# Last block of a four-layer perceiver kernel: the last four batches' state-space preparation moved ahead of the perceptron, its weight bytes loaded early

## The chip, the cores and the metric

The kernel runs on one core of a Trainium2 chip. A core has a matrix engine (TensorE, PE in the profile, with PEld for its weight loads), VectorE (DVE), ScalarE (ACT), GpSimd (POOL) and SyncE (SP), which here only issues DMAs. Each engine works through its own instruction list in the order in which the program puts it there, and waits for others through semaphores. Matmuls write PSUM; the other engines read it and move results to SBUF. The metric is device time in microseconds (us), lower is better.

## The reference, cut to what matters

Sixteen batches of 64 tokens with 256 features (x) go through four layers. Each has a cross-attention on a context of 1024 keys with 192 features, a second mixer and a feed-forward part. The change lies in the last layer:

```python
x = x + _L3_xattn_ref(_layernorm(x, axis=-1), ctx_768, ...)
x = x + _L3_attn_ref(_layernorm(x, axis=-1), ...)
x = x + _L3_ffn_ref(_layernorm(x, axis=-1), L3_ffn_k0, L3_ffn_k1, L3_ffn_k2, ...)
```

Its second mixer is a selective state space (Mamba style) on 512 channels with 16 states each:

```python
u, x_gate = jnp.split(x @ in_proj_w, 2, axis=-1)
u = silu(conv3(u) + conv_b)
delta, b, c = jnp.split(u @ x_proj_w, [512, 528], axis=-1)
delta = softplus(delta @ dt_proj_w + dt_proj_b)
h = jnp.exp(d_t[:, :, None] * a) * h + d_t[:, :, None] * b_t[:, None, :] * u_t[:, :, None]
y_t = jnp.einsum('bds,bs->bd', h, c_t)
y = (y + u * D_param) * silu(x_gate)
return y @ out_proj_w
```

Its feed-forward part is a perceptron whose weights are given as booleans, one byte each, meaning +1 or -1: 256 features, doubled to (x, -x), to 1024, to 1024, to 256, with relu between and a scale per layer.

## The kernel before

Tokens lie on partitions in eight tiles of 128, and `xs` holds the running x in SBUF. In the last layer three pieces of work are interleaved by hand in the order in which the program records them; PE's order is kept exactly (`manual_schedule`), that of the other engines is set by the framework from the recorded order.

- **Cross-attention**: `heads64` (L420). It first forms `wvo` from `wvT` and `wo` in `output_matrices`, and does not read `wvT` and `wo` again. It then goes through (tile, batch, group of heads); at each step it calls `breathe` four times, which here is the state space's `go`. After tile i's output, `finished(i)` sets `ssm.ready`.
- **State space**: `state_space` (L1797). A chunk is four batches, 256 tokens, two tiles, so there are four chunks, 0 to 3. `prepare(k)` is a generator: layer norm (`os`), transposes (`hTs`), eight input projections with a three-tap convolution on DVE (`up`, `ug`), Silu, the projections for b and c (`bc`) and for the step size (`du`, four of them: "dt"), then softplus, the product delta times u on POOL (L1897), and a write of both to HBM (`dus`). `items(k)` then reads them back replicated on partitions (`rep`, `bc_rep`) and does 32 items, in eight slots of four: ACT makes the decay `da` (L1938), DVE multiplies (L1944), scans (L1948) and multiplies (L1951) into one of six `x` buffers. After each slot, PE sums over the states with 16 matmuls (`add_up`, L1972); after every second slot DVE applies D and the gate (`v`, L1978). The chunk ends with an output projection added to `xs` (L89). Chunk 3 can be prepared only when the attention of the last tile is finished.
- **Perceptron**: `dense_setup` (L2009) turns the bytes into fp32 weights: w0 and w2 on DVE, w1 in eight pieces on ACT (L2021). `dense(first, 2)` does two tiles: norm and transposes (`o`, `hT`), first layer in eight groups of matmuls (`ps_h`, weights w0), second in eight groups of eight-deep matmuls (w1), third (w2) added to `xs` (L2061) and written out. Relus alternate between ACT (L2033) and DVE (L2031). It yields 15 times: 1, 4, 8 and 2.

`go` runs one piece of the current preparation, then as many items as `credit` allows: each call adds `rate`, 1.1 during the attention and 1.5 during the perceptron. After the attention `L3` (L1765) calls `dense` for tiles 0, 2, 4 and 6, with one `go` after each yield, and before each calls `go` until those tiles' state space is done:

```python
for i in range(0, NT, 2):
    while ssm.done < i + 2:
        ssm.go()
    for _ in dense(i, 2):
        ssm.go()
```

Weights come through a ring of two buffers of 7296 fp32 per partition, in the order of `packs`. The bytes of the perceptron are the last pack (`pack_L3_ffn`, L1755), whose buffer is the one that the attention's weights hold until its end; its three DMAs are issued on SP's queue. The state space's weights (`weights`, L1834) are loaded near the start of the layer.

Of the kernel before, what the change touches and what calls it, by code (L numbers as in the profile page):

```python
# [13 lines left out]
U8 = mybir.dt.uint8  # L14
AF = mybir.ActivationFunctionType
ALU = mybir.AluOpType
# [3 lines left out]
B, S, D = 16, 64, 256  # L20
# [12 lines left out]
RING = 7296  # L33
# [9 lines left out]
class Net:  # L43
# [376 lines left out]
    def heads64(  # L420
# [4 lines left out]

        nc = self.nc
        wq, wkT, wvT, wo, bo, wvo, wvo2 = self.pack()
        large = large or self.misc
        self.n_pT = 3
        qpT, hT = {}, {}  # L430
# [1318 lines left out]
    def pack_L3_attn(self):  # L1749

        self.slot()
        shape = {n: self.a[f"L3a_{n}"].shape for n in ("in", "bc", "out")}
        return self.carve(*shape["in"]), self.carve(128, 4, 512), self.carve(*shape["bc"]), self.carve(*shape["out"])

    def pack_L3_ffn(self):  # L1755
        t = self.ring.tile([128, 4 * RING], U8, tag="w", name="w")
        got, at = [], 0
        for name, c, f in (("L3f_k0", 4, 1024), ("L3f_k1", 8, 1024), ("L3f_k2", 8, D)):
            v = t[:, at : at + c * f].rearrange("p (c f) -> p c f", f=f)
            at += c * f  # L1760
            self.nc.sync.dma_start(v, self.a[name])
            got.append(v)
        return got

    def L3(self, ctx_pool):  # L1765
        tc, nc = self.tc, self.nc
        with ExitStack() as stack:

            def pool(name, **kw):
                return stack.enter_context(tc.tile_pool(name=name, reuse_waits="tile", **kw))  # L1770

            self.sb = pool("sb_L3a", bufs=1, side="right")
            ps = pool("ps_halves", bufs=1, space=PSUM)
            banks = [ps.tile([128, 2, 256], F32, name=f"halves{n}") for n in range(2)]
            self.halves, self.halves_y = ([t[:, h, :] for t in banks] for h in range(2))
            stack.enter_context(tc.manual_schedule(engines={mybir.EngineType.PE}))
            ssm = self.state_space()
            with (
                tc.tile_pool(name="sb_L3x", bufs=1, side="left", reuse_waits="tile") as self.lp,
                tc.tile_pool(name="ps_L3x", bufs=1, space=PSUM, reuse_waits="tile") as self.lps,  # L1780
            ):
                self.heads64(
                    lambda shape: self.lps.tile(shape, F32, tag="t", bufs=2, name="large"),
                    ssm.go, ssm.more, ssm.first,
                )
            ctx_pool.__exit__(None, None, None)
            self.lp = pool("sb_L3f", bufs=1, side="left")
            self.lps = pool("ps_L3f", bufs=1, space=PSUM)
            ssm.rate = 1.5
            dense = self.dense_setup()  # L1790
            for i in range(0, NT, 2):
                while ssm.done < i + 2:
                    ssm.go()
                for _ in dense(i, 2):
                    ssm.go()

    def state_space(self):  # L1797
        nc = self.nc
        N = 16
        w = []  # L1800
        s = SimpleNamespace(ready=0, done=0, rate=1.1, credit=0.0, prepared=0, started=0)
        al = self.sb.tile([128, 4 * N], F32, name="al")
        at = VEC_AT["L3a_A"]
# [30 lines left out]
        def weights():  # L1834
            for n, to in zip(("in", "bc", "out"), (w[0], w[2], w[3])):
                nc.sync.dma_start(to, self.a[f"L3a_{n}"])
            yield

        def prepare(k):
            win, wdt, wbc, _ = w  # L1840
            ug = ugs[k % 2]
            os = []
            for t in range(2):
# [1 line left out]
                mv, rs = self.norm_tile(x, 1e-5)  # L1845
                os.append(self.sb.tile([128, D], F32, tag="os", bufs=2, name="os"))
                nc.vector.tensor_scalar(os[t], x, mv[:, 0:1], rs, ALU.subtract, ALU.mult)
            yield
            hT = self.sb.tile([128, 2, CHUNK], F32, tag="hTs", name="hTs")
            for t in range(2):  # L1850
                nc.scalar.copy(hT[:, :, t * 128 : (t + 1) * 128], self.transposed(os[t]))
            yield
            up = self.act.tile([128, 4, 4, S + 2], F32, tag="hT", name="up")
            nc.gpsimd.memset(up[:, :, :, 0:1], 0.0)
            nc.gpsimd.memset(up[:, :, :, S + 1 : S + 2], 0.0)
# [16 lines left out]
                if m % 2:  # L1872
                    yield
            nc.scalar.activation(ug, ug, AF.Silu)
            yield
            yield
            ps = self.misc([32, CHUNK])
            self.mm(ps, [(wbc[:, c, :], ug[:, c, :]) for c in range(4)])
            bc = self.sb.tile([32, CHUNK], F32, tag="bc", name="bc")
# [100 lines left out]

        s.prep, s.work = weights(), None

        def go(place=None):

            if s.prep is None and s.prepared < NC and s.ready >= 2 * s.prepared + 2 and s.prepared <= s.done // 2 + 1:
                s.prep = prepare(s.prepared)
            if s.prep is not None and next(s.prep, s) is s:
                s.prepared += s.prep.gi_code is prepare.__code__
                s.prep = None
            if s.work is None and s.started < s.prepared:  # L1990
                s.work = items(s.started)
                s.started += 1
            self.spare_dve = s.work is not None
            s.credit = min(s.credit + s.rate, 2 * s.rate)
            while s.work is not None and s.credit >= 1:
                s.credit -= 1
                if next(s.work, s) is s:
                    s.work = None
# [9 lines left out]

    def dense_setup(self):  # L2009
        nc = self.nc  # L2010
        k0, k1, k2 = self.pack()

        w0 = self.lp.tile([128, 2, 1024], F32, name="w0")
        w1 = self.lp.tile([128, 8, 1024], F32, name="w1")
        w2 = self.lp.tile([128, 8, D], F32, name="w2")
        for c in range(2):
            nc.vector.tensor_tensor(w0[:, c, :], k0[:, c, :], k0[:, 2 + c, :], ALU.subtract)
        minus = self.lp.tile([128, 1], F32, name="minus")
        nc.vector.memset(minus, -1.0)
        for c in range(8):  # L2020
            nc.scalar.activation(w1[:, c, :], k1[:, c, :], AF.Identity, bias=minus, scale=2.0)  # L2021
        nc.vector.tensor_scalar(w2, k2, 2.0, -1.0, ALU.mult, ALU.add)

        sc = self.lp.tile([128, 3], F32, name="sc")
        nc.sync.dma_start(sc, self.a["L3f_s"].partition_broadcast(128))
        nc.vector.tensor_scalar(sc, sc, 2.0, None, ALU.mult)
        out = self.a["out"].rearrange("(i p) d -> p i d", p=128)

        def relu(n, out, ps, k):
            if n % 2:  # L2030
                nc.vector.tensor_scalar(out, ps, sc[:, k : k + 1], 0.0, ALU.mult, ALU.max)  # L2031
            else:
                nc.scalar.activation(out, ps, AF.Relu, scale=sc[:, k : k + 1])  # L2033

        def dense(first, tiles):
            hT = self.lp.tile([128, 2, CHUNK], F32, tag="hT", bufs=1, name="hT")
            for t in range(tiles):
                x = self.xs[:, first + t, :]
                mv, rs = self.norm_tile(x, 1e-5)
                o = self.lp.tile([128, D], F32, tag="o", bufs=2, name="o")  # L2040
                nc.vector.tensor_scalar(o, x, mv[:, 0:1], rs, ALU.subtract, ALU.mult)
                self.evict(hT[:, :, t * 128 : (t + 1) * 128], self.transposed(o))
            yield

            def layer(name, w, x, chunks, k):
                r = self.lp.tile([128, 8, CHUNK], F32, tag=name, bufs=1, name=name)
                for m in range(8):
                    ps = self.lps.tile([128, CHUNK], F32, tag="h", bufs=4, name="ps_h")
                    self.mm(ps, [(w[:, c, m * 128 : (m + 1) * 128], x[:, c, :]) for c in range(chunks)])
                    relu(m, r[:, m, :], ps, k)  # L2050
                    if m % 2 or chunks > 2:
                        yield
                return r

            r0 = yield from layer("r0", w0, hT, 2, 0)
            r1 = yield from layer("r1", w1, r0, 8, 1)
            for t in range(tiles):
                i = first + t
                po = self.misc([128, D])
                self.mm(po, [(r1[:, m, t * 128 : (t + 1) * 128], w2[:, m, :]) for m in range(8)])  # L2060
                nc.vector.scalar_tensor_tensor(  # L2061
                    self.xs[:, i, :], po, sc[:, 2:3], self.xs[:, i, :], ALU.mult, ALU.add
                )
                nc.sync.dma_start(out[:, i, :], self.xs[:, i, :])
                yield

        return dense

# [59 lines left out]
    def run(self, layers):  # L2128
# [6 lines left out]
            "L1_ffn": (self.L1_ffn, [self.pack_L1_gate]),  # L2135
            "L2_xattn_attn": (self.L2_xattn_attn, [lambda: self.pack_heads64("L2"), self.pack_L2_attn]),
            "L2_ffn": (self.L2_ffn, [self.pack_L2_gate] + [lambda e=e: self.pack_L2_expert(e) for e in range(E)]),
            "L3": (None, [lambda: self.pack_heads64("L3"), self.pack_L3_attn, self.pack_L3_ffn]),
        }
        self.packs = [p for l in layers for p in plan[l][1]]  # L2140
        self.loaded, self.at, self.ctx_n = {}, 0, 0
# [186 lines left out]
```

## Time and profile before

| | us |
|---|---|
| three runs, median (lowest to highest) | 2994.78 (2992.84 to 3002.1) |
| profiled execution | 2998.29 |
| its span, first to last instruction | 2996.5 |
| last layer's attention ends on PE | 2734.35 |
| last matmul ends | 2993.2 |
| instructions | 42608 |

The profile is of one execution. Its page gives busy time by engine (part 1), the span in 40 slices (2) and the costliest groups of instructions (5); the trace can be asked for stretches of time, waits, and lists in order of time. "Granted clock" is the share of its full clock that PE ran at. In lists of instructions a row reads: start, length, engine, line, operation, written tile <- read tiles, shape, count, and in brackets the idle time before it and what ended it. An fp32 matmul that the program wrote appears as two.

The line numbers L69, L179 and L89 belong to helpers: L69 is every ordinary matmul, L179 a transpose, L89 an addition to `xs`. The tile names tell them apart: `ps_h` is the perceptron's first two layers, `halves` everything else of the last layer.

### The profile page before, as it was taken

The page shows a single profiled execution, that of the slowest core. Times are in us where ns is not written, and L with a number is a line of the kernel's source. Part 1 is how long each engine was busy: PE and PEld are TensorE (multiplying, and loading weights), DVE is VectorE, ACT ScalarE, POOL GpSimd, SP SyncE. Part 2 cuts the span into 40 slices and gives each one's busy share as a digit, 9 for nine tenths or more (in the row PEclk, how much of TensorE's full clock was granted, in tenths as well). Part 3 has the DMA queues.
Part 4 walks back from the last instruction along what each step waited for, and adds up shares of the span by engine and source line. Part 5 has one row for each costly group of instructions (what it writes and reads, how often), then busy time and mean ns, then how long its engine had stood idle before and what let it go on. Part 6 is the DMA issues. An engine that isn't in the chain of part 4 may idle for free. (4 is left out here: it accounts for less than half of the span.)

```text
span 2996.5 us, 42608 instructions
## 1 busy us (share of the span) xinstructions
PE 2700.2 (90%) x16840; PEld 1952.8 (65%) x16840; DVE 1482.1 (49%) x3177; ACT 1022.7 (34%) x2290; POOL 308.7 (10%) x428
## 2 busy tenths in 40 slices
PE   7888997999999788989999998898998898897899
PEld 3566784666666345867777776795776666665668
DVE  3654114666666653234444444314445747658581
ACT  2331122555555211222333322122334455445330
POOL 1112223000000111310101001101001000000000
PEclk9987997999999897989999999899999999998999
DMA  9503771101101003831121112551112222121210
GB/s 241 177 27 144 263 239 50 40 26 32 30 26 33 29 8 135 294 76 46 45 66 45 43 58 70 199 212 63 52 51 88 64 62 73 57 68 53 57 36 7
DMA packets 79220, 253.55 MB, mean 85 GB/s; under 512 B 15151, under 2 KB 26954, under 8 KB 69290
## 3 DMA queue, kind: packets, MB, share of 16 engines
q1 hardware_dynamic: 59562, 165.01, 17.7%
q0 software_dynamic: 13312, 80.28, 7.9%
q10 hardware_dynamic: 6144, 5.51, 0.5%
q8 instruction: 134, 2.20, 0.3%
q14 instruction: 68, 0.56, 0.1%
HBM read 233.80 MB, written 14.82 MB: 83 GB/s over the span
## 5 line engine op out<-in xcount | busy, mean ns | idle before, releaser
L223 DVE TENSOR_REDUCE nmx<-sc 128x1 f32<-128x1024 f32 x264 | 311.8, 1219 | 219.6 <-PE sc L507 134.6
L225 ACT ACTIVATE p<-sc,nmx 128x1024 f32<-128x1024 f32 x264 | 294.6, 1116 | 316.9 <-DVE nmx L223 316.2
L507 PE MATMUL sc<-ctxT,qp 128*128 128x512 f32 (+1 forms) x1024 | 356.0, 602 | 0.0
L507 PEld LDWEIGHTS sc<-ctxT,qp 128*128 128x128 f32 (+1 forms) x1024 | 139.0, 190 | 154.0 <-issue 153.4
L69 PE MATMUL halves<-ctx,pT 128*128 128x192 f32 x1024 | 191.6, 344 | 9.4 <-DVE xs L89 4.0
L69 PEld LDWEIGHTS halves<-ctx,pT 128*128 128x128 f32 x1024 | 179.1, 203 | 12.3 <-DVE xs L89 4.5
L160 POOL TENSOR_TENSOR ln_rs<-ln_ve,nhalf 128x1 f32<-128x1 f32 x120 | 66.9, 562 | 1134.1 <-DVE ln_ve L158 1025.5
L69 PE MATMUL misc<-ctx,pT 128*128 128x192 f32 x1024 | 177.6, 327 | 0.5 <-DVE qT L472 0.5
L235 PE MATMUL ps_t<-ident,p 128*128 128x128 f32 x1088 | 147.8, 278 | 25.3 <-ACT p L225 17.7
L69 PEld LDWEIGHTS misc<-ctx,pT 128*128 128x128 f32 x1024 | 166.3, 191 | 2.1 <-DVE qT L472 1.0
L1938 ACT ACTIVATE da<-rep,al 128x252 f32<-128x252 f32 x256 | 114.7, 498 | 114.8 <-DVE x L1948 98.4
L235 PEld LDWEIGHTS ps_t<-ident,p 128*128 128x128 f32 x1088 | 127.7, 143 | 39.2 <-ACT p L225 22.5
L1948 DVE TENSOR_TENSOR_SCAN x<-da,x 128x512 f32<-128x512 f32 x128 | 152.1, 1213 | 1.9 <-ACT da L1938 1.4
L235 PE MATMUL misc<-ident,p 128*128 128x128 f32 x1024 | 139.8, 283 | 14.2 <-ACT p L225 6.7
L237 ACT COPY pT<-ps_t 128x512 f32<-128x512 f32 x182 | 104.3, 585 | 140.5 <-PE ps_t L235 138.5
L235 PEld LDWEIGHTS misc<-ident,p 128*128 128x128 f32 x1024 | 112.2, 143 | 40.3 <-ACT p L225 13.3
L69 PE MATMUL ps_h<-r,w 128*128 128x256 f32 x512 | 115.3, 385 | 0.0
L237 ACT COPY pT<-misc 128x512 f32<-128x512 f32 x128 | 75.0, 586 | 114.9 <-PE misc L235 114.6
L69 PEld LDWEIGHTS ps_h<-r,w 128*128 128x128 f32 x512 | 97.8, 192 | 16.6 <-issue 2.9
L69 PE MATMUL gu<-dT,wa 128*128 128x128 f32 (+1 forms) x864 | 104.8, 280 | 3.7 <-ACT dT L64 2.4
L239 DVE COPY pT<-misc 128x512 f32<-128x512 f32 x128 | 88.2, 689 | 39.4 <-PE misc L235 28.9
L69 PE MATMUL po<-wb,hid 128*128 128x256 f32 (+1 forms) x440 | 105.6, 387 | 0.0
(472 smaller groups left out, 4437.7 us busy)
## 6 DMA issues: line engine op xcount, KB each, us to landing
ctx<-in_ctx SPq DMA_DIRECT2D x48, 768.0 KB, 4.4
ctxT<-in_ctxT SPq DMA_DIRECT2D x48, 512.0 KB, 4.0
w<-in_L2f_W SPq DMA_DIRECT2D x24, 1024.0 KB, 8.5
rep<-dus SPq DMA_DIRECT2D x256, 64.0 KB, 1.9
ctxT<-in_ctxT SPq DMA_DIRECT2D x16, 768.0 KB, 12.9
ctxT<-in_ctxT SPq DMA_DIRECT2D x96, 128.0 KB, 3.5
ys<-yb ACTq DMA_DIRECT2D x40, 128.0 KB, 4.4
bc_rep<-bcs SPq DMA_DIRECT2D x32, 128.0 KB, 3.0
```

Source lines behind the costliest of these rows:

```text
L69: self.nc.tensor.matmul(out, lhsT, rhs, start=n == 0, stop=n == len(pairs) - 1)
L160: nc.gpsimd.tensor_tensor(rs, ve, self.nhalf, ALU.pow)
L223: self.nc.vector.tensor_reduce(nmx, sc, AX.X, ALU.max, negate=True)
L225: self.nc.scalar.activation(p, sc, AF.Exp, bias=nmx, accum_out=sums)
L235: self.nc.tensor.transpose(ps[:, u, :], p[:, at : at + 128], self.ident)
L237: self.nc.scalar.copy(pT[:, 4 * g : 4 * g + 4, :], ps)
L239: self.nc.vector.tensor_copy(pT[:, 0:4, :], ps)
L507: nc.tensor.matmul(sc[u][:, bass.ts(kh, 512)], qp[n][par][rows, h : h + 2, :].rearrange("p h q -> p (h q)"), ctx[0][rows, at], start=n == ...
L1938: nc.scalar.activation(da[:, g, :, 1:], now[j][:, 0, :].rearrange("p (b s) -> p b s", s=S)[:, :, 1:], AF.Exp, scale=al[:, col : col + 1],)
L1948: nc.vector.tensor_tensor_scan(flat, da.rearrange("p g b s -> p (g b s)"), flat, 0.0, ALU.mult, ALU.add)
```

## The change

- `heads64` remembers `wo` and `wvT` as `spent`. The perceptron's bytes are no longer a pack of the ring: `fetch_L3_ffn` loads them, as a second piece of `weights`, so near the start of the layer: k0 into `wo`'s room, k2 into `wvT`'s, k1 into a new room (8 x 256 fp32) at the end of the state space's buffer, which this fills.
- `go` takes a `share` and `hurry`. With `hurry=2` it runs two pieces of a preparation instead of one, unless the first ends with `WAIT`; four places of `prepare` yield it. During the attention `hurry` is 1.
- After the attention `go` is called twice with `hurry=2` before the perceptron's weights are made, then after every yield.
- The rate of items is 1.4 instead of 1.5, and each yield of `dense` passes a share of it: 0.3 after the norm, 0.5 per two groups of the first layer, 1.0 otherwise.
- Half of w1's eight pieces are converted on DVE instead of ACT.

```diff
@@ heads64
         wq, wkT, wvT, wo, bo, wvo, wvo2 = self.pack()
+        self.spent = wo, wvT
@@ pack_L3_attn
-        return self.carve(*shape["in"]), self.carve(128, 4, 512), self.carve(*shape["bc"]), self.carve(*shape["out"])
+        got = self.carve(*shape["in"]), self.carve(128, 4, 512), self.carve(*shape["bc"]), self.carve(*shape["out"])
+        return *got, self.carve(128, 8, 256)
 
-    def pack_L3_ffn(self):
-        t = self.ring.tile([128, 4 * RING], U8, tag="w", name="w")
-        got, at = [], 0
-        for name, c, f in (("L3f_k0", 4, 1024), ("L3f_k1", 8, 1024), ("L3f_k2", 8, D)):
-            v = t[:, at : at + c * f].rearrange("p (c f) -> p c f", f=f)
-            at += c * f
+    def fetch_L3_ffn(self, room):
+        got = []
+        for (name, f), to in zip((("L3f_k0", 1024), ("L3f_k1", 1024), ("L3f_k2", D)), room):
+            c = self.a[name].shape[1]
+            v = to.rearrange("p c f -> p (c f)").bitcast(U8)[:, : c * f].rearrange("p (c f) -> p c f", f=f)
             self.nc.sync.dma_start(v, self.a[name])
             got.append(v)
         return got
@@ L3
-                    ssm.go, ssm.more, ssm.first,
+                    lambda place: ssm.go(), ssm.more, ssm.first,
...
-            ssm.rate = 1.5
+            ssm.rate = 1.4
+            for _ in range(2):
+                ssm.go(hurry=2)
             dense = self.dense_setup()
             for i in range(0, NT, 2):
                 while ssm.done < i + 2:
-                    ssm.go()
-                for _ in dense(i, 2):
-                    ssm.go()
+                    ssm.go(hurry=2)
+                for share in dense(i, 2):
+                    ssm.go(share, hurry=2)
@@ state_space
+        WAIT = "more would have to wait"
@@ weights
             yield
+            self.ffn = self.fetch_L3_ffn((self.spent[0], w[4], self.spent[1]))
+            yield
@@ prepare: after os, after hTs, and twice after Silu
-            yield
+            yield WAIT
@@ go
-        def go(place=None):
-            if s.prep is None and s.prepared < NC and s.ready >= 2 * s.prepared + 2 and s.prepared <= s.done // 2 + 1:
-                s.prep = prepare(s.prepared)
-            if s.prep is not None and next(s.prep, s) is s:
-                s.prepared += s.prep.gi_code is prepare.__code__
-                s.prep = None
+        def go(share=1.0, hurry=1):
+            for _ in range(hurry):
+                if s.prep is None and s.prepared < NC and s.ready >= 2 * s.prepared + 2 and s.prepared <= s.done // 2 + 1:
+                    s.prep = prepare(s.prepared)
+                got = None if s.prep is None else next(s.prep, s)
+                if got is s:
+                    s.prepared += s.prep.gi_code is prepare.__code__
+                    s.prep = None
+                if got is WAIT:
+                    break
...
-            s.credit = min(s.credit + s.rate, 2 * s.rate)
+            s.credit = min(s.credit + share * s.rate, 2 * s.rate)
@@ dense_setup
-        k0, k1, k2 = self.pack()
+        k0, k1, k2 = self.ffn
...
         for c in range(8):
-            nc.scalar.activation(w1[:, c, :], k1[:, c, :], AF.Identity, bias=minus, scale=2.0)
+            if c % 2:
+                nc.vector.tensor_scalar(w1[:, c, :], k1[:, c, :], 2.0, -1.0, ALU.mult, ALU.add)
+            else:
+                nc.scalar.activation(w1[:, c, :], k1[:, c, :], AF.Identity, bias=minus, scale=2.0)
@@ dense
-            yield
+            yield 0.3
...
-                    if m % 2 or chunks > 2:
-                        yield
+                    if m % 2 or chunks > 2:
+                        yield min(1.0, chunks / 4)
...
-                yield
+                yield 1.0
@@ run
-            "L3": (None, [lambda: self.pack_heads64("L3"), self.pack_L3_attn, self.pack_L3_ffn]),
+            "L3": (None, [lambda: self.pack_heads64("L3"), self.pack_L3_attn]),
```

More of the change, by code (lines that the diff above doesn't have):

```diff
@@ L1837, in weights @@
             yield
+            self.ffn = self.fetch_L3_ffn((self.spent[0], w[4], self.spent[1]))
+            yield
         def prepare(k):
-            win, wdt, wbc, _ = w
+            win, wdt, wbc, *_ = w
             ug = ugs[k % 2]
@@ L1851, in prepare @@
                 nc.scalar.copy(hT[:, :, t * 128 : (t + 1) * 128], self.transposed(os[t]))
-            yield
+            yield WAIT
             up = self.act.tile([128, 4, 4, S + 2], F32, tag="hT", name="up")
@@ L1874, in prepare @@
             nc.scalar.activation(ug, ug, AF.Silu)
-            yield
-            yield
+            yield WAIT
+            yield WAIT
             ps = self.misc([32, CHUNK])
@@ L2042, in dense @@
                 self.evict(hT[:, :, t * 128 : (t + 1) * 128], self.transposed(o))
-            yield
+            yield 0.3
             def layer(name, w, x, chunks, k):
@@ L2051, in layer @@
                     if m % 2 or chunks > 2:
-                        yield
+                        yield min(1.0, chunks / 4)
                 return r
@@ L2064, in dense @@
                 nc.sync.dma_start(out[:, i, :], self.xs[:, i, :])
-                yield
+                yield 1.0
         return dense
```

## The prediction

> **What bounds the kernel now.** I read busy time first, then TensorE (PE) in stages from the end of the last cross-attention, then who PE waited for, then the chain of waits around the longest gap.
>
> The page, part 1, busy us, share and instructions of each engine:
>
> ```profile
> PE 2700.2 (90%) x16840; PEld 1952.8 (65%) x16840; DVE 1482.1 (49%) x3177; ACT 1022.7 (34%) x2290; POOL 308.7 (10%) x428
> ```
>
> PE is busy 90% of the span, so a change can only win PE's idle time and slow matmuls. The stages after the attention (start:end, length, busy of PE, PEld, DVE, ACT, POOL with counts, granted clock, DMA share, GB/s):
>
> ```profile
> 2734.35:2753.60 19.25, 8.46 (x34) 4.58 (x33) 13.27 (x29) 11.80 (x17) 2.02 (x3) 0.70 0.27 99
> 2753.60:2803.00 49.40, 48.94 (x240) 38.70 (x241) 32.77 (x56) 17.48 (x34) 0.11 (x1) 0.98 0.12 33
> 2803.00:2829.00 26.00, 20.12 (x93) 16.96 (x92) 8.02 (x16) 8.38 (x13) 3.81 (x6) 0.97 0.24 76
> 2829.00:2915.00 86.00, 73.36 (x364) 53.16 (x364) 81.39 (x113) 32.71 (x76) 0.00 (x0) 0.91 0.17 45
> 2915.00:2951.50 36.50, 35.66 (x166) 30.80 (x164) 7.25 (x19) 1.80 (x4) 1.10 (x2) 1.00 0.02 5
> ```
>
> Three kinds of time: a start in which nobody is busy (PE 8.5 of 19 us), a stretch where VectorE (DVE) has little to do (8 of 26 us), then one where DVE is the bound (81 of 86) and PE waits; after 2915 PE alone has work. What PE waited for in this tail (for what, us, times, longest):
>
> ```profile
> PE halves L1972 <- DVE x L1951: 15.6, 5, 8.0
> PE ps_h L69 <- DVE w L2017: 4.1, 1, 4.1
> PE halves L1972 <- ACT hTs L1851: 3.7, 1, 3.7
> PE halves L179 <- DVE o L2041: 2.9, 1, 2.9
> PE halves L179 <- DVE xs L2061: 2.8, 3, 2.1
> ```
>
> 15.6 us are add-ups (L1972) waiting for the scans of chunk 3, the last four batches. Why they were late, from the chain of waits (start, us, what):
>
> ```profile
> 2814.63 1.06 ACT du L1892
> 2815.71 1.28 ACT L1893
> 2817.00 1.16 ACT du L1893
> 2818.18 1.24 DVE du L1894
> 2819.42 0.07 issue
> 2819.49 2.83 POOL du L1897 x4
> ...
> 2826.56 1.93 DMA rep<-dus
> ```
>
> Chunk 3's preparation ends only here, so its 32 scan items of 2.33 us (0.60 + 1.13 + 0.60, start to start: multiply, scan, multiply) start at 2829 and DVE needs 2829 to 2914 for them. And idle PE costs twice:
>
> ```profile
> 2742.19 3.62 PE L69 MATMUL ps_h<-hT,w 128*128 128x256 f32 x8 [4.14 <-DVE w L2017]
> ...
> 2831.94 1.06 PE L1972 MATMUL halves<-x,stack 128*32 128x256 f32 x2 [7.99 <-DVE x L1951]
> 2836.58 3.62 PE L1972 MATMUL halves<-x,stack 128*32 128x256 f32 x14 [3.58 <-DVE x L1951]
> ```
>
> Eight such matmuls take 1.89 us elsewhere, here 3.62: after an idle stretch of some 4 us the next 3.6 us run at half clock, worth 1.7 us.
>
> **The sum.** PE's idle from 2734.4 on is 30.6 us by its timeline: 10.8 before 2753.6 and 19.8 after (0.46 + 0.36 + 0.46 + 7.99 + 3.58 + 2.49 + 2.05 + 1.35 + 0.23 + 0.36 + 0.51). All PE work stays: the instruction order of the changed program has the same matmuls, placed elsewhere, and is unchanged up to the end of the attention. So I walk that order with durations of this trace and compare idle time.
>
> *Bytes early.* Three DMAs, 1.84 MB, leave the SP queue at 2734.4 (where the chain shows 5.71 us of waiting for them) and stand behind L1836's loads at 2021.8. SP then waits from 2022.3 to 2065.5 for a context buffer anyway; the second and third DMA wait for the last of the output_matrices matmuls (2027.7), and queued behind them are only the context loads that wait till 2065.5. Cost nothing on SP. On the DMA engines: the last expert's results (ys<-yb, issued 2022.7) must land before the gathers (2029.16) whose norm gives the first tile to PE; that o was ready at 2037.45 and PE took it at 2041.55: 4.1 us of cover, given by the 14 us of w_dt matmuls. The skill (Trainium Kernel Development and Optimization, Key Constraints) says DMAs issued from SP, ACT and POOL share the same 16 engines and interleave: by that, 1 MB at the 400 GB/s or so seen for these weights at 2735 adds 2.6 us; by the row (ys<-yb landed fine beside 1.6 MB of other weights), nothing. Both are under 4.1, I take 0. Ends: 0 and +3 (all 4.6 us of bytes ahead, and gathers slowed from 2.7 us to twice that, less cover).
>
> *Start.* PE ends the attention at 2734.35 in both. The DMA wait goes, but the conversions stay and DVE gets more: half of w1 (four pieces; no row has it, w2 of 2048 columns took 1.22, so 0.6 each; above it 1.05 as on ACT). DVE in the new order: xs 2736.5, scan, norm, two w0 pieces (1.14 each), os at 2741.7; then w1 2.3, w2 1.1, norms and one scan item, o of dense's two tiles at 2748.3 and 2749.7. PE: idle until 2742.2, then os transposes and an add-up, idle from 2744.6 or 2746 to 2748.5, transposes, idle 1, in_proj from 2750.2, at half clock for some 2 us. Before, at 2753.6, PE had done os, o, that add-up and 1.9 us of dense; in the new order it has the first three and 1.9 us of in_proj at about 2753.4. ACT loses 4 of its 8 pieces (4.2 us of 8.42), but nothing starts on that now. Gain 0: a DMA wait becomes a wait for DVE's queue. Ends -4 and +3.
>
> *Preparation ahead.* Its matmuls (in_proj 8, bc 1, dt 4, about 0.93 us each, 12 us) come before most of the first dense block instead of between its pieces; the last dt ends at 2780.6 rather than 2813.4. Then the same chain: ACT's Exp/Ln behind three scan-paced da pairs, 2787.5; DVE's add 2788.7; POOL; first rep 9 us after POOL's start as before, 2798. On DVE stand before chunk 3's first item the rest of chunk 2 and its last v, which waits for an add-up that PE reaches at 2802: items start at 2803, 26 us earlier. bc_rep must wait for chunk 2's last item (2793.8), 7 us to landing: 2800.5, covered by the same v.
>
> New stalls that I find: 0.5 (relus that stand behind Silu on ACT release ps_h tiles late), 1.0 (out-projection right behind its add-up), 1.6 at the first dense boundary, 2.5 at the second (the residual add xs, whose PSUM tile the next transposes need, queues behind scan work; 2.05 before), 0.85 at the third (xs and hT, as before). Sum 6.45 in place of 19.8: gain 13.4.
>
> Chunk 3's 75 us of items then have from 2803 to 2906 on DVE, with relus and the rest about 90 of 103 us: DVE is no longer the bound, PE is.
>
> *Half clock.* The rows after 2829 that ran slow (2 for 1.06, 14 for 3.62, 24 for 5.81, 48 for 12.31) hold about 5 us over full speed; with gaps of 1 to 2.5 us in their place I let 0.5 stay. Gain 4.5.
>
> *POOL beside scans.* In every row of before POOL's four du multiplies (0.72 each) ran while DVE was idle or reading PSUM; now they lie beside multiplies and scans that read two SBUF tensors. The skill (SBUF — State Buffer, section SBUF: two separate sides) speaks against this: GpSimd and VectorE share one pair of ports under an exclusive lock, so either blocks for a whole instruction of the other. By the row the chain costs 2.8 us, by the rule up to 4 x 1.13 = 4.5 more for POOL, and 2.9 for DVE. First rep is 4 to 5 us ahead of its use, so I take 0, end +1.
>
> Sum: 0 + 0 + 13.4 + 4.5 = 18. Against the profiled execution (span 2996.5, time 2998.3) that is 2978.5 of span; against the median of 2994.8, **2977**.
>
> **Rivals.**
> - *All gaps shrink more* (0.15): my walk with full-speed matmuls alone ends at a span of 2972, 25 us less: 2970.
> - *The win is mostly handed back at the start and the boundaries* (0.18). For it: PE idle of 7.6 us at 2734 is longer than any now, DVE's order there is fixed, and 4 us more at the start plus 2 us at four places with their half clock leave about 5: 2990. Against: each of these waits I have seen placed in the order and priced.
> - *Slower: DVE's fixed order makes PE wait in each slot* (0.12). Relus stand between scan items in DVE's queue, and PE's next dense matmul or add-up waits for them. If in each of the 11 remaining slots PE waits one item, 2.33 us, that is 25.6 us, and 2977 becomes 3003. It decides from 18/11 = 1.6 us a slot. For: this happened before at 2849 (2.49), 2904 (1.35). Against: there DVE was 95% busy, now about 87%, and four ps_h tiles let PE run ahead.
> - *The change does nothing*: excluded as far as the order goes, the last dt stands behind two pieces of the second layer in place of eight.
>
> **Numbers.** Forecast 0.55 (2971 to 2985). A change under 0.3%, 9 us, can't be told from none here: faster 0.55 + 0.15 + 0.03 of the second rival, same 0.15, slower 0.12. The range reaches from 2964 to 2992: it leaves out the slower rival and a little on both sides.
>
> **What would show it.** Right: PE's wait for x in the add-ups falls from 15.6 to under 5 us; chunk 3's first item at about 2803; granted clock in the later stages near 1.0; about 7.6 us of PE idle at 2734 with no DMA in it; no loss at 2029 to 2042. Wrong: PE waiting for relus (r) or xs at every slot, first item after 2815, or the start over 23 us up to the same work.

## The result and the profile after

The changed kernel takes 2979.64 us (median of 5 runs, 2978.99 to 2982.0), the kernel before beside it 2997.28 (5 runs, 2992.84 to 3004.89): ratio 0.994, 95% interval 0.9922 to 0.9958. That is 17.6 us less; 18 were forecast. The profiled execution took 2981.61, its span is 2979.8. The page, part 1:

```profile
PE 2695.6 (90%) x16840; PEld 1950.6 (65%) x16840; DVE 1484.7 (50%) x3181; ACT 1018.0 (34%) x2286; POOL 311.3 (10%) x428
```

PE's busy time fell by 4.6 us of the same 16840 matmuls, the rest of the gain is idle time. The stages of the tail after the attention, which here ends at 2737.2 (columns as before: start:end, length, busy PE, PEld, DVE, ACT, POOL, granted clock, DMA share, GB/s):

```profile
2737.20:2754.10 16.90, 5.66 (x24) 2.32 (x23) 15.63 (x31) 7.98 (x13) 3.92 (x3) 0.62 0.06 16
2754.10:2811.30 57.20, 56.12 (x270) 44.69 (x269) 36.49 (x63) 25.45 (x47) 4.77 (x6) 0.96 0.19 56
2811.30:2915.00 103.70, 99.43 (x507) 79.34 (x507) 88.60 (x133) 33.99 (x78) 1.07 (x2) 1.00 0.14 39
2915.00:2977.00 62.00, 60.72 (x288) 51.68 (x286) 10.49 (x26) 4.63 (x10) 1.10 (x2) 1.00 0.02 7
```

The start is still a hole (PE 5.7 of 16.9 us), now with DVE busy through 15.6 of it. In the third row, chunk 3's scans, PE is busy 96% at a clock of 1.00, where before it was 73.36 of 86 us at 0.91; DVE is at 85%. The last row is PE alone: 62 us, where before 78. What PE waited for from 2734 on:

```profile
PE halves L179 <- DVE minus L2034: 7.7, 1, 7.7
PE halves L179 <- DVE xs L2079: 3.1, 3, 1.4
PE halves L179 <- DVE ln_ve L158: 2.0, 1, 2.0
PE ps_h L69 <- ACT hT L64: 1.4, 3, 0.5
PE halves L1982 <- ACT du L1900: 1.1, 1, 1.1
PE halves L179 <- DVE o L2059: 0.8, 1, 0.8
```

The 15.6 us of add-ups waiting for `x` are gone; no line of the list names `x`. The largest wait is one at the start. The "minus" in it is a memset that the profile names because it ran about then; PE needed `os`, which DVE finished just before it.

One caution for what follows. The attention's end fell anywhere from 2726.3 to 2737.2 in the profiles of this study, so whole spans are compared by medians, and stages by the tail: from the attention's end to the last matmul's. It is 258.9 us before (the 255.9 that some expectations name left out its last 3 us) and 239.4 after. Tails repeat less well than idle time: two profiles of the changed kernel had 239.4 and 243.3, with 17.4 and 18.0 us of idle PE. Most of the difference is in two rows of matmuls that ran slowly in the second; they are shown in the last section.

### The profile page after: what moved, and what is told of

It reads as the page before. It is cut to its first block, busy times and chain, and to the rows that moved or that the text cites. A ratio compares the mean times of both kernels' runs of the same rounds, so it can differ in the third digit from the quotient of the medians.

```text
span 2979.8 us, 42598 instructions
## 1 busy us (share of the span) xinstructions
PE 2695.6 (90%) x16840; PEld 1950.6 (65%) x16840; DVE 1484.7 (50%) x3181; ACT 1018.0 (34%) x2286; POOL 311.3 (10%) x428
## 5 line engine op out<-in xcount | busy, mean ns | idle before, releaser
L69 PE MATMUL misc<-ctx,pT 128*128 128x192 f32 x1024 | 177.6, 327 | 0.6 <-DVE qT L473 0.6
L237 ACT COPY pT<-misc 128x512 f32<-128x512 f32 x128 | 74.9, 586 | 115.1 <-PE misc L235 114.8
## 6 DMA issues: line engine op xcount, KB each, us to landing
ctxT<-in_ctxT SPq DMA_DIRECT2D x16, 768.0 KB, 13.2
```

What stands on the lines that cost most here:

```text
L69: self.nc.tensor.matmul(out, lhsT, rhs, start=n == 0, stop=n == len(pairs) - 1)
L237: self.nc.scalar.copy(pT[:, 4 * g : 4 * g + 4, :], ps)
```

## Experiments

All times are medians of 5 runs (6 for e4 and e6, 7 for e3, 11 for e7) with the kernel before run beside them on the same chip. The readings of all profiles together, in us: PE idle in the first 24 us of the tail ("start") and in the rest; when chunk 3's first and last scan start, counted from the attention's end; what is left of the tail after that last scan.

| kernel | ahead | pace | ratio (95% interval) | idle start | idle rest | scans of chunk 3 | left after |
|---|---|---|---|---|---|---|---|
| before | no | old | 1 | 10.8 | 19.8 | 94.6 to 177.9 | 81.0 |
| changed | yes | new | 0.994 (0.9922 to 0.9958) | 11.3 | 6.2 | 75.7 to 174.8 | 64.6 |
| e11, changed again | yes | new | 0.9949 (0.9934 to 0.9964) | 11.8 | 6.2 | 76.3 to 178.7 | 64.6 |
| e1_no_ahead | no | new | 0.9936 (0.992 to 0.9953) | 9.3 | 10.1 | 88.9 to 179.1 | 62.5 |
| e2_old_pace | yes | old | 0.9953 (0.9936 to 0.9969) | 11.8 | 10.0 | 74.9 to 157.0 | 90.5 |
| e3_ahead_only | yes | old | 0.9963 (0.9948 to 0.9978) | 13.6 | 9.9 | 78.8 to 160.1 | 90.1 |
| e4_bytes_late | yes | new | 0.9947 (0.9932 to 0.9963) | 11.7 | 6.2 | 76.7 to 177.5 | 64.6 |
| e5_pace_only | no | new | 0.9936 (0.9923 to 0.9949) | 9.0 | 10.1 | 88.2 to 179.9 | 62.4 |
| e6_low_rate | no | 1.15 | 0.9952 (0.9937 to 0.9967) | 9.6 | 10.7 | 88.4 to 176.6 | 65.8 |
| e7_neither | no | old | 0.9988 (0.9978 to 0.9999) | 9.8 | 19.8 | 91.8 to 174.8 | 81.0 |
| e8_norm_first | yes | new | 0.9915 (0.99 to 0.9929) | 6.6 | 6.6 | 69.1 to 169.9 | 64.6 |
| e12, the same | yes | new | 0.9916 (0.9902 to 0.9931) | 6.6 | 6.6 | 69.1 to 169.8 | 64.6 |
| e9_norm_no_ahead | no | new | 0.9959 (0.9945 to 0.9972) | 7.5 | 10.1 | 89.5 to 179.7 | 62.5 |
| e10_w1_on_act | yes | new | 0.995 (0.9936 to 0.9964) | 12.2 | 6.2 | 76.9 to 177.6 | 64.6 |

"Pace" is the number of items that the program records beside one dense block of two tiles: before 15 yields x 1.5 = 22.5, changed 1.4 x (0.3 + 4 x 0.5 + 8 + 2) = 17.2.

### Taking parts away: e1 to e4

My theory was that preparation ahead makes the gain, because chunk 3's scans start earlier; the rival, that the slower pace makes it.

**e1_no_ahead**: the changed kernel without the two early calls and with one piece of preparation a call.

```diff
-            for _ in range(2):
-                ssm.go(hurry=2)
             dense = self.dense_setup()
...
-                    ssm.go(hurry=2)
+                    ssm.go(hurry=1)
-                    ssm.go(share, hurry=2)
+                    ssm.go(share, hurry=1)
```

> The changed kernel without its preparation ahead: no two calls of go before the weights are made, one piece per call (hurry 1); bytes early, w1 shared and pace kept. Theory (the gain is chunk 3's preparation finished sooner, so that its scans start before VectorE becomes the bound): the gain is gone, ratio to before 0.998 to 1.003, first item of chunk 3 again 90 us or more after the attention's end (92.6 before, 74.3 changed) and PE waiting 10 us or more for x in the add-ups. Rival (the slower pace, fewer scan items between dense pieces, keeps PE fed): most of the gain stays, ratio 0.994 to 0.996. Rival (early bytes and shared w1 conversion): ratio 0.994 to 0.996 too, with the start shorter.

2981.89 us, ratio 0.9936. My theory missed, the rival of the pace held: the gain stayed whole (a little more than its 0.994 to 0.996) although the first item of chunk 3 came at 86.7 us after the attention's end, against 74.2 in the changed kernel and 92.6 before. PE's waits (here after 2732):

```profile
PE halves L179 <- DVE o L2057: 11.5, 3, 8.8
PE halves L179 <- DVE xs L2077: 2.4, 2, 2.1
PE ps_h L69 <- ACT hT L64: 1.4, 3, 0.5
PE halves L69 <- DVE v L1986: 1.4, 1, 1.4
```

No `x` here either: scans that start 12 us later than in the changed kernel starve nobody.

**e2_old_pace**: the changed kernel with the old pace.

```diff
-            ssm.rate = 1.4
+            ssm.rate = 1.5
...
-                    ssm.go(share, hurry=2)
+                    ssm.go(1.0, hurry=2)
```

> The changed kernel with the pace of before: rate 1.5, each yield a full share. Theory (preparation ahead): ratio 0.993 to 0.997, chunk 3's first item as early as in the changed kernel or a few us earlier, but some waits of PE for x come back because items are queued faster than VectorE does them (2.33 us each): 2 to 8 us. Rival (pace): the gain is gone, 0.999 to 1.002.

2985.89 us, ratio 0.9953. Most of the gain stays here too. One wait for `x` of 1.7 us is back, and two of 3.0 and 2.5 us in which an add-up's PSUM waits for `xs` (L2079), DVE's addition that stands behind scan work.

**e3_ahead_only**: the kernel before with the two early calls and `hurry=2`; bytes late, w1 on ACT, rate 1.5.

```diff
             ssm.rate = 1.5
+            for _ in range(2):
+                ssm.go(hurry=2)
             dense = self.dense_setup()
...
-                    ssm.go()
+                    ssm.go(hurry=2)
```

> The kernel before with the preparation ahead alone: the two calls of go with hurry 2 before the weights are made and two pieces per call; bytes late, w1 on ScalarE, rate 1.5 without shares. Theory: most of the gain, ratio 0.995 to 0.998 (start 2 to 6 us longer than in the changed kernel, since the bytes' wait of 5.7 us is back). Rival (pace, or bytes): 0.999 to 1.004.

2987.36 us, ratio 0.9963. Its waits for `x` and `xs` after the start are those of e2. In the table, e2 and e3 finish their scans 18 to 21 us earlier than the kernel before and then have 90 us of PE work left alone. An early end of the scans is worth only the idle time that goes with it, here 10 us: the rest of what PE did not do beside them it does after them.

**e4_bytes_late**: the changed kernel with the bytes in the ring as before.

```diff
-            self.ffn = self.fetch_L3_ffn((self.spent[0], w[4], self.spent[1]))
-            yield
...
-        k0, k1, k2 = self.ffn
+        k0, k1, k2 = self.pack()
...
-            "L3": (None, [lambda: self.pack_heads64("L3"), self.pack_L3_attn]),
+            "L3": (None, [lambda: self.pack_heads64("L3"), self.pack_L3_attn, self.pack_L3_ffn]),
```

> The changed kernel with the bytes loaded as before, as the last pack of the ring, so after the attention. The prediction's step (the DMA wait was replaced by a wait for VectorE's queue, so early bytes are worth little): VectorE needs the bytes at about 5 us after the attention's end and they land at about 6 to 8, so 1 to 4 us lost, ratio 0.9945 to 0.996. Rival (early bytes carry the gain): 5 to 8 us or more lost, 0.996 to 0.998, with a DMA wait on VectorE of 4 us or more at the start.

2983.61 us, ratio 0.9947: not to be told from the changed kernel. The idle of the start is the same 11.7 us, cut differently (waits of 6.0 and 5.0 in place of 7.7 and 2.0). Bringing the bytes early removed a DMA wait under which DVE's work would have stood anyway.

### The pace by itself: e5 to e7

**e5_pace_only**: the kernel before with the new pace and nothing else.

```diff
-            ssm.rate = 1.5
+            ssm.rate = 1.4
...
-                for _ in dense(i, 2):
-                    ssm.go()
+                for share in dense(i, 2):
+                    ssm.go(share=share)
...
-            s.credit = min(s.credit + s.rate, 2 * s.rate)
+            s.credit = min(s.credit + share * s.rate, 2 * s.rate)
@@ dense: its three kinds of yield
-            yield
+            yield 0.3
...
-                        yield
+                        yield min(1.0, chunks / 4)
...
-                yield
+                yield 1.0
```

> The kernel before with the new pace alone (rate 1.4 and a share for each slot); bytes late, w1 on ACT, no preparation ahead. Pace theory (fewer items recorded in each dense block keep dense work beside the scans, so PE stops waiting for x): PE's waits for x fall from 15.6 us to under 4, the first item of chunk 3 comes 85 to 95 us after the attention's end as before, the tail from the attention's end to the last matmul is 242 to 248 us instead of 255.9, ratio 0.994 to 0.997. Rival (pace needs the early bytes too, because the start decides how many slots are left): waits for x stay above 8 us, ratio 0.998 to 1.001.

2981.07 us, ratio 0.9936: as the pace theory said and a little better, with a tail of 242.3 (its 242 to 248 left out the 3 us named above). No wait for `x` is left. This is the whole gain of the change from its smallest part. Its stages, counted from the attention's end at 2736.6:

```profile
2736.60:2754.00 17.40, 8.47 (x33) 6.32 (x34) 12.28 (x28) 12.54 (x19) 2.02 (x3) 0.80 0.30 109
2754.00:2822.00 68.00, 64.65 (x325) 51.14 (x323) 40.13 (x68) 21.96 (x39) 4.06 (x6) 1.00 0.16 47
2822.00:2915.00 93.00, 89.90 (x454) 70.10 (x454) 81.37 (x116) 37.22 (x84) 0.00 (x0) 0.98 0.17 46
2915.00:2979.00 64.00, 60.16 (x276) 50.58 (x276) 13.54 (x30) 4.53 (x10) 1.10 (x2) 0.97 0.02 7
```

The third row is the one to set beside the row 2829:2915 of before. DVE does the same work (81.37 against 81.39 us), but in 93 us rather than 86, and PE's share of that stretch rises from 85% to 97%, because the program has put more dense matmuls beside the same scans. PE in order of time where chunk 3's first add-up stands, before and in e5:

```profile
2821.95 1.99 PE L69 MATMUL ps_h<-hT,w 128*128 128x256 f32 x8 [0.46 <-ACT hT L64]
2831.94 1.06 PE L1972 MATMUL halves<-x,stack 128*32 128x256 f32 x2 [7.99 <-DVE x L1951]
```

```profile
2822.57 7.83 PE L69 MATMUL ps_h<-hT,w 128*128 128x256 f32 x32 [0.46 <-ACT hT L64]
2830.23 7.07 PE L69 MATMUL ps_h<-r,w 128*128 128x256 f32 x32
2837.23 1.92 PE L1972 MATMUL halves<-x,stack 128*32 128x256 f32 x16
```

Before, only 8 matmuls of the dense block stand ahead of the add-up, and PE waits 8 us for `x`; in e5 it has 64 to do first, and `x` is there when it arrives.

**e6_low_rate**: the kernel before with one number changed, 17.25 items a block, spread evenly.

```diff
-            ssm.rate = 1.5
+            ssm.rate = 1.15
```

> The kernel before with ssm.rate 1.15 in place of 1.5 in every slot, no shares: 17.25 items for each dense block, as the new pace gives, but spread evenly over the slots. If the number of items in a block is what counts: like e5_pace_only, waits for x under 4 us, ratio 0.994 to 0.997. If their distribution over the slots counts (few items in slots with little PE work): PE waits in the short slots instead (r or xs, 5 us or more), ratio 0.998 to 1.003.

2982.32 us, ratio 0.9952: the number of items is what counts. The shares for short slots add at most a little: two waits for `x` (1.75 and 1.05 us) that e5 does not have.

**e7_neither**: the changed kernel with neither the preparation ahead nor the new pace (the edits of e1 and e2 together).

> The changed kernel with neither the preparation ahead nor the new pace: only the early bytes and the shared w1 conversion stay. If these two are the only causes of the gain and replace one another: PE's waits for x are back at 10 us or more, PE idle in the tail 26 to 31 us, ratio 0.998 to 1.001. If early bytes alone bring chunk 3 ahead enough: waits for x under 6 us, ratio 0.994 to 0.997.

2993.76 us, ratio 0.9988 (0.9978 to 0.9999). PE's waits (after 2734):

```profile
PE halves L1980 <- DVE x L1959: 15.6, 5, 8.0
PE halves L179 <- DVE o L2057: 8.8, 1, 8.8
PE halves L179 <- DVE xs L2077: 2.8, 3, 2.1
```

The first line is that of the kernel before to the tenth. So the early bytes and the shared w1 are worth some 4 us together (0 to 7 by the interval), and the two other parts carry the rest: either alone takes the idle after the start from 19.8 to 10, both take it to 6.

### The start: e8 to e12

**e8_norm_first**: the changed kernel, with the first dense block's norm and transposes recorded ahead of the early calls, and the conversions of the weights after them.

```diff
+            dense, rest = self.dense_setup()
+            start = dense(0, 2)
+            share = next(start)
             for _ in range(2):
                 ssm.go(hurry=2)
-            dense = self.dense_setup()
+            rest()
+            ssm.go(share, hurry=2)
...
-                for share in dense(i, 2):
+                for share in dense(i, 2) if i else start:
@@ dense_setup: the conversions of w0, w1 and w2 move into rest()
```

> The changed kernel with the first dense block's norm and transposes recorded ahead of preparation and of the weights' conversions, to shorten the start. If the start is bound by DVE's order: PE's idle in the start falls from 11.3 us to 6 to 8, ratio 0.992 to 0.9935. If something else bounds it (the w0 conversion and the last attention rows must come anyway): idle stays at 10 to 12 us, ratio as after, 0.994.

2971.19 us, ratio 0.9915, faster than both kernels. PE in order of time from the attention's end, first the changed kernel, then e8:

```profile
2745.08 0.69 PE L179 MATMUL halves<-ident,os 128*128 128x128 f32 x2 [7.68 <-DVE minus L2034]
2746.54 3.63 PE L1982 MATMUL halves<-x,stack 128*32 128x256 f32 x16 [0.77 <-ACT hTs L1861]
2752.14 0.69 PE L179 MATMUL halves<-ident,o 128*128 128x128 f32 x2 [1.97 <-DVE ln_ve L158]
2753.65 0.69 PE L179 MATMUL halves<-ident,o 128*128 128x128 f32 x2 [0.83 <-DVE o L2059]
2754.14 5.72 PE L69 MATMUL halves<-hTs,w 128*128 128x256 f32 x16
```

```profile
2734.59 0.76 PE L179 MATMUL halves<-ident,o 128*128 128x128 f32 x4 [2.94 <-DVE o L2065]
2735.85 0.68 PE L179 MATMUL halves<-ident,os 128*128 128x128 f32 x2 [0.50 <-ACT hT L64]
2739.23 0.66 PE L179 MATMUL halves<-ident,os 128*128 128x128 f32 x2 [2.70 <-DVE os L1861]
2740.36 3.07 PE L1986 MATMUL halves<-x,stack 128*32 128x256 f32 x16 [0.46 <-ACT hTs L1865]
2743.35 3.72 PE L69 MATMUL halves<-hTs,w 128*128 128x256 f32 x16
```

The in_proj matmuls start 11.7 us after the attention's end (2731.64) instead of 17.0, and find the clock up: 3.72 us for 16, where the changed kernel's took 5.72. `os` is hardly earlier (PE has its second half 7.6 us after the attention's end, 7.9 in the changed kernel); what differs is `o`. DVE's order in the changed kernel, from the attention's last `xs`:

```profile
2739.31 0.41 DVE L89 TENSOR_TENSOR xs<-xs,halves 128x256 f32<-128x256 f32 x1
...
2742.95 1.21 DVE L2032 TENSOR_TENSOR w<-w 128x1024 f32<-128x1024 uint8 x1
2744.61 0.41 DVE L1857 TENSOR_SCALAR os<-xs,ln_mv,ln_rs 128x256 f32<-128x256 f32 x1 [0.45 <-POOL ln_rs L160]
...
2747.36 1.22 DVE L2040 TENSOR_SCALAR w<-w 128x2048 f32<-128x2048 uint8 x1
...
2751.67 0.41 DVE L2059 TENSOR_SCALAR o<-xs,ln_mv,ln_rs 128x256 f32<-128x256 f32 x1 [0.38 <-POOL ln_rs L160]
```

The first `o` stands behind w0, `os`, w1, w2 and a scan item, 12.4 us after `xs`; in e8 it comes 0.3 us after `xs`, as it did in the kernel before (2736.83 after 2736.49), so that PE does its transposes in the hole and in_proj follows the add-up without a wait. The conversions were not urgent: PE first reads w0 at 2759.70.

**e9_norm_no_ahead**: e8 without the preparation ahead (e1's edit).

> e8_norm_first without the preparation ahead: one step of preparation for each slot as in the kernel before; the new pace, the early bytes, the shared w1 and the order of e8's start stay. If the pace and the short start make up e8's gain and preparation ahead adds what it added to the changed kernel (some 2 us of tail, e1 against after): tail 235 to 239 us, idle 13 to 17, ratio 0.9915 to 0.9935. If preparation ahead is what fills PE in the start of e8 (in_proj right behind the first add-up): PE waits for w0 or os again there, idle 18 or more, ratio 0.9935 to 0.996.

2984.59 us, ratio 0.9959: my first expectation missed, and the rival's ratio was met. Of its 4.4 us more idle than e8's only 0.9 are in the start, where the rival looked for it (PE waits 3.8 us for `os`); 3.5 are in the rest, at the block boundaries. Its tail is 242.2 us, e8's 234.5. But its profile was of its fastest run (2973.54, the others 2983.21 to 2985.59), so what makes those others 10 us longer is not in a trace; nor is why e9, with less idle than e1, has the worse ratio. That stays open. What e8 against e9 does show is that preparation ahead, which added nothing to the changed kernel that its time could show, counts once the start is short: the two intervals do not touch.

**e10_w1_on_act**: the changed kernel with all of w1 converted on ACT.

```diff
-            if c % 2:
-                nc.vector.tensor_scalar(w1[:, c, :], k1[:, c, :], 2.0, -1.0, ALU.mult, ALU.add)
-            else:
-                nc.scalar.activation(w1[:, c, :], k1[:, c, :], AF.Identity, bias=minus, scale=2.0)
+            nc.scalar.activation(w1[:, c, :], k1[:, c, :], AF.Identity, bias=minus, scale=2.0)
```

> The changed kernel with all eight pieces of w1's conversion on ACT. If DVE is the bound of the start: 2.8 us of pieces leave DVE's queue ahead of the norms that PE waits for there, the idle of the start falls from 11.3 to 8 to 10 us, ratio 0.992 to 0.994. Rival (ACT's longer queue, 8.4 us of pieces, holds up the evictions of in_proj and of the dense tiles): idle of the start 12 us or more, ratio 0.994 to 0.997.

2980.27 us, ratio 0.995, as the rival said: PE no longer waits 2.8 us for `o` but 3.7 for `hT`, whose eviction stands behind w1 on ACT. Sharing w1 exchanges one wait for another. But the first expectation was not given its chance: ACT's first piece waited 3.29 us for the memset of `minus` (L2034), which it reads and which DVE does only after w0 and `os`. Without that wait `hT` would come some 3 us earlier (an estimate from the trace of e10), about what the first expectation asked for; no run moves the memset.

**e11_changed_again** and **e12_norm_first_again** repeat the changed kernel and e8. The record has e8 and e12 on the same chip number, 0, and e11 on 12.

> The changed kernel once more, beside e9 and e10 on one chip. If its 0.994 is right and e8_norm_first's lead is real: 0.993 to 0.995, outside e8's interval of 0.990 to 0.993. If e8's lead was chance: 0.992 or below.

> e8_norm_first once more, on another chip, since its lead over the changed kernel (0.9915 against 0.994 and 0.9949) is no wider than the spread of single runs. If the lead is real: ratio 0.990 to 0.993, PE idle in the tail 13 to 14 us as in e8. If it was chance: 0.994 or above.

0.9949 (0.9934 to 0.9964) and 0.9916 (0.9902 to 0.9931). Each came out where its first run did, and the two intervals do not touch: e8's lead of some 8 us is real.

## Why the prediction was right, and where it was not

- **The sum.** Forecast: 13.4 us of idle and 4.5 of half clock. Measured in the tail: 13.2 of idle (30.6 to 17.4; 12.6 in the second profile) and 6.3 of busy time (258.9 - 30.6 = 228.3 against 222.0; 2.9 in the second profile). The size was right because the recorded order of the changed program was walked, and that order holds every part of the change. That the total came within half a us is luck: the tail shrank by 19.5 us in one profile and by 15.6 in the other, and of half clock, where 0.5 us was allowed to stay, the first profile shows none after the start and the second 3.4.
- **Preparation ahead** is the step whose reason failed. It said that items start "26 us earlier" (24, if both are counted at the first multiply, which before was at 2826.94) and that the gain follows. They started 18 us earlier (74.2 against 92.6 after the attention's end), and this is not what the gain needs: e5, with 6 us, has all of it. An earlier start does end most of the waits for `x` by itself (e3, 0.9963), but it is one way of two. The new rate and shares, of which the prediction did not speak, were in the walked order and their effect was put down to the earlier start. The cause is how much dense work lies beside the scans: 32 items, 75 us of DVE, recorded at 22.5 a block lie beside some 1.4 dense blocks; DVE is then the bound and PE is left 81 us alone afterwards. At 17 a block they lie beside 1.9, need 88 to 102 us from first scan to last, and PE has work in nearly all of it.
- **Its durations.** The last dt matmul was forecast 46.3 us after the attention's end and ended at 52.1. Of the 5.8, 1.1 are the later in_proj and about 1 is its first 16 matmuls (5.72 us instead of 3.62, a loss of 2.1, of which I had allowed half); up to 1.1 is the wait for `du`. The rest is not traced. The first item is late by 5.5 us.
- **Start, gain 0.** Idle 11.3 against 10.8, the first wait 7.68 against 7.6 forecast. Right, and for the reason given: a wait for bytes became a wait for DVE's queue. What I did not draw from it is that DVE's order was then the thing to change; e8 gets 5 us there.
- **Bytes early, cost 0.** The gathers started at 2034.51 instead of 2029.16. 3.2 us of that are a shift that was there before the bytes (the transposes behind them, 2044.76 against 2041.55, show it alone), so 2.2 us are theirs. The Trainium skill's rule (Trainium Kernel Development and Optimization, Key Constraints: all queues share the 16 engines) gave an estimate of 2.6, the row nothing: the rule was the nearer one, and the cover of 4.1 us hid it.
- **New stalls.** 6.45 forecast, 6.2 measured: 1.8 at the first boundary (forecast 1.6), 1.9 at the second (2.5), 0.8 at the third (0.85), 0.6 before an output projection (1.0), and one of 1.1 for `du` on ACT in place of 0.5 for a relu.
- **POOL beside scans, taken as 0.** The slowing that the Trainium skill's lock (SBUF — State Buffer, SBUF: two separate sides) would give is there, off the path, and it was to be seen in the kernel before: there, beside POOL's four multiplies (from 2819.49), DVE was not only idle or reading PSUM, as the prediction read it, but did two norms from SBUF in 1.55 us, 0.41 each elsewhere:

```profile
2820.91 1.55 DVE L2041 TENSOR_SCALAR o<-xs,ln_mv,ln_rs 128x256 f32<-128x256 f32 x2
```

POOL's four multiplies in the changed kernel, 2.83 us before, and DVE's rows beside them:

```profile
2796.50 3.67 POOL L1907 TENSOR_TENSOR du<-du,ug 128x256 f32<-128x256 f32 x4 [27.01 <-DVE du L1904]
```

```profile
2797.20 2.38 DVE L1954 TENSOR_TENSOR x<-rep,bc_rep 128x512 f32<-128x512 f32 x2 [0.39 <-PE halves L1982]
2799.51 2.86 DVE L1958 TENSOR_TENSOR_SCAN x<-da,x 128x512 f32<-128x512 f32 x2
...
2810.49 0.48 DVE L1988 SCALAR_TENSOR_TENSOR v<-ug,vecs,halves 128x256 f32<-128x256 f32 x1 [4.83 <-PE halves L1982]
```

POOL lost 0.8 us (up to 4.5 in the prediction's estimate), DVE 1.1 in two multiplies (1.28 elsewhere) and 0.5 in two scans (2.33 elsewhere), 1.6 in all (2.9 in the estimate). It is the estimate that was too large, not the rule: taken one by one, the instructions end in turn (POOL at 2797.90, DVE 2798.45, POOL 2799.03, DVE 2799.59, POOL 2800.17), each 0.55 to 0.58 us after the one before, where alone they take 0.6 to 0.7: each waited for one whole instruction of the other, as the rule says. POOL met two multiplies, not four scans. Nobody missed the time: chunk 3 could not begin before `v` at 2810.49, which waited 4.8 us for PE.

- **Rivals.** That DVE's fixed order makes PE wait in each slot did not happen: the idle after the start is 6.2 us in all, not 25.6. The rival in which the start hands the win back was the nearest miss: the start gave nothing, but took nothing either.

## What to carry to other kernels

Where two engines share a stage by a hand-written interleave, count the work of the bound engine that is recorded beside each block of the other, and aim to make them last equally long. Here 22.5 items are 52 us of DVE and 17.2 are 40, beside a dense block that PE does in 42 when it has nothing else (the last one before, 2951.5 to 2993.2). No run tried fewer than 17.2. One number (1.5 to 1.15) was worth as much here as moving a whole preparation. Scans that end earlier help only if the other engine has less to do after them. When several parts of a change are walked through one instruction order, a right sum says nothing of which part made it; only undoing each alone does.

## What the runs showed of the hardware

A gap shorter than expected can cost the clock, and does so in one run and not in the next. After waits of 2.5 to 3 us, 16 add-up matmuls that take 1.92 us took 3.5 (e2, after 2.95) and 3.3 (e2, after 2.53), but 1.92 in e3 after the same 2.53. Even gaps of 1.3 and 1.4 us at a block boundary, with 0.46 more behind the transposes, did it. The same two rows of the changed kernel, in its first profile and in its second (e11):

```profile
2826.91 7.17 PE L69 MATMUL ps_h<-hT,w 128*128 128x256 f32 x32 [0.46 <-ACT hT L64]
2880.01 3.72 PE L69 MATMUL ps_h<-hT,w 128*128 128x256 f32 x16 [0.46 <-ACT hT L64]
```

```profile
2822.86 8.86 PE L69 MATMUL ps_h<-hT,w 128*128 128x256 f32 x32 [0.46 <-ACT hT L64]
2877.65 5.41 PE L69 MATMUL ps_h<-hT,w 128*128 128x256 f32 x16 [0.46 <-ACT hT L64]
```

The granted clock is 1.00 in both rows of the first; in the second it is 0.55 in the first 3.5 us of the one and 0.67 over the other. The 5.41 is there in e4, e8, e10 and e12 too. What decides it stays open. The slow stretch can also outlast the 3.6 us seen before: in e10, after 3.7 us of idle, 16 matmuls of in_proj took 6.94 us, where e8's took 3.72.

GpSimd was slowed in one-column work too: POOL's ln_rs, 0.55 us alone, took 1.46 beside DVE's second w0 conversion and 1.53 beside a scan in the start of the changed kernel. DVE's scan there kept its length (1.23 us, 1.22 elsewhere), but its norms, and PE behind them, waited for POOL: the 0.45 and 0.38 us in brackets in the list of DVE's order.
